# Row statistics moved from VectorE to additions and to ScalarE, and closer due times for the last graphs, in a planned four-layer graph network

## The chip, the core and the metric

The kernel runs on one core of a Trainium2 chip. The metric is the device time of one execution in microseconds (us). Before the change it is 2857.97 us, the median of three runs (2857.74 to 2859.51).

## The reference

There are 64 graphs. Each has 256 nodes with 512 features (`x`) and a 256 x 256 matrix of weights between nodes (`adj`), all float32. Every graph passes four layers, and each layer normalizes the rows of x, takes the positive part, and adds what the layer gives to x:

```
h = max(layernorm(x), 0);  x = x + L0(h, adj, W, a)      # attention, elu
h = max(layernorm(x), 0);  x = x + L1(h, adj, kernel, bias)
h = max(layernorm(x), 0);  x = x + L2(h, adj, kernel)
h = max(layernorm(x), 0);  x = x + L3(h, adj, W)
layernorm(x) = (x - mean) / sqrt(var + 1e-5)             # along a row
L0: e = leaky_relu(Wh1 + Wh2^T); att = softmax(where(adj > 0.5, e, -9e15), axis=1); elu(att @ Wh)
L1: An = dh * (adj + I) * dh, dh = 1/sqrt(rowsum(adj + I)); relu(An @ h @ kernel + bias)
L2: relu(adj @ h @ kernel) * mask, mask = 1 where a row of h has an entry that isn't 0
L3: agg = adj @ h / max(rowsum(adj), 1e-6); relu([h, agg] @ W^T)
```

## The kernel before, in words

A graph's 256 rows lie in two chunks of 128 partitions, so x is a tile `xs` of [128, 2, 512]. Its four quarters have keys of their own (`xs.00` to `xs.11`: chunk, then half of the columns).

Nothing in the source fixes the order of the work by loops alone. `graph(b)` (L341) only records operations: an engine, an estimated time, the keys it reads and writes, and a due time. A graph's last operations are due at `APART * b` (L343), and `Plan.place` (L69) walks back from there, so that each operation gets the due time that its heirs leave it. Then the planner places all operations one by one. Each engine takes the operation that can start first, then an urgent one, then the one that is due first. The estimates are multiplied by `STRETCH` (L25), a step from one engine to another is charged `HOP` = 0.25 us, and PE counts an operation as startable only `SPARE` (L26) after its operands are ready in the plan. Buffers are limited by the table at L782: seven tiles of x, three of h, eight banks of PSUM and so on. The operations are then emitted in the order of their planned starts, and on the chip every engine runs its own queue in that order. All transfers are issued from SP's queue.

Around that plan, the work of one graph is as follows.

- **Loads.** x and `a_nat`, the adjacency by rows (L367, L369), and the same adjacency in eight block transfers as `ab` (L567), from which VectorE (DVE) makes the transposed `aT` (L570).
- **Norm** (L372). For each chunk DVE takes `bn_stats` (L381) and `bn_aggr` (L383). GpSimd (POOL) adds the epsilon and takes the power -1/2 (L385, L387). DVE scales by the degree factor where asked (L390) and makes the bias `nb` (L392). ScalarE (ACT) writes `h` as a relu with scale and bias (L396).
- **Degrees** (L576 to L583). DVE sums `a_nat` by rows, POOL makes `dh`, DVE makes `rdeg`.
- **Attention.** DVE takes the logits as products with `wa` (L590), which is made once, at the start, from W and the two halves of `a` (L252 to L282). One half of the logits goes through DRAM and comes back spread along the rows as `pl` (L354 to L362). ACT adds the two (L596). DVE makes `off`, -9e15 where the adjacency is at most 0.5 (L601), the leaky relu (L603), the product with the comparison (L605), the sum with `off` (L607) and the negated row maximum (L610). ACT takes the exponential with its row sum (L614), DVE the reciprocal (L617) and the scaling of each chunk (L620).
- **Products.** `aggregate` (L424) multiplies h with the adjacency on TensorE (PE) into `pt`, the copies of which make seven left operands (L414 to L407). `project` (L485) takes seven products in three banks `pz`, `py`, `pv` (L503), with ACT copies (L542) and DVE additions (L544) out of PSUM between them. In the last layer there are two such projections, and h is transposed first: DVE turns blocks (L722), and 16 transfers put them in place as `hw` (L727).
- **Additions to x.** `elu0` (L626), `relu_add` (L669) and `masked` (L699) add a layer's result to x in three pieces: quarter 10, quarter 11 and the whole chunk 0.
- **Store** of x (L770).

At the start the weights come in as well. For the last layer PE transposes them (L325), and ACT copies them out of PSUM (L332); POOL makes sums of weights (L289).

Of the kernel before, what the change touches and what calls it, by code (L numbers as in the profile page):

```python
# [10 lines left out]
AF = mybir.ActivationFunctionType  # L11
ALU = mybir.AluOpType
AX = mybir.AxisListType

P = 128
Q = 32
BANK = 512
EPS_LN = 1e-5
EPS_DEG = 1e-6
ALPHA = 0.2  # L20
NEG_INF = -9000000000000000.0
HOP = 0.25
APART = 12.0

STRETCH = {"DVE": 1.06, "ACT": 1.1, "POOL": 1.1, "PE": 1.0, "DMA": 1.0}  # L25
SPARE = 0.8  # L26

# [121 lines left out]
def kernel(  # L149
# [21 lines left out]
    nc = tc.nc  # L171
    B, N, F = x.shape
    O = w0.shape[1]
    NC = N // P
# [14 lines left out]
    class Tiles:  # L189
# [5 lines left out]
        def declare(self, name, shape, pool=None, tag=None):  # L195
            tag = pool or tag or name
            self.tiles[name] = Buffered(shape, tag, f"{name}_{self.name}")
# [140 lines left out]
    def quarter(t, i, j):  # L338
        return t[:, i, j * OH : (j + 1) * OH]

    def graph(b):  # L341

        me = Tiles(str(b), APART * b)  # L343
        op, declare, together = me.op, me.declare, me.together

        def along(name, column, keys):
# [22 lines left out]
        op("DMA", 256, lambda g: nc.sync.dma_start(  # L369
            g["a_nat"], adj[b].rearrange("(c p) m -> p c m", p=P)), (), ["a_nat"])  # L370

        def norm(l, scale=None):  # L372

            st, mv, rs, nb, h = (f"{n}{l}" for n in ("stats", "mv", "rstd", "nb", "h"))
            declare(st, [P, NC, 6], tag="stats")
            declare(mv, [P, NC, 2], tag="mv")
            declare(rs, [P, NC], tag="rstd")
            declare(nb, [P, NC], tag="nb")
            declare(h, [P, NC, F], tag="h")
            for c in range(NC):  # L380
                op("DVE", 0.69, lambda g, c=c: nc.vector.bn_stats(g[st][:, c, :], g["xs"][:, c, :]),  # L381
                   XS[2 * c : 2 * c + 2], [f"{st}.{c}"])
                op("DVE", 0.18, lambda g, c=c: nc.vector.bn_aggr(g[mv][:, c, :], g[st][:, c, :]),  # L383
                   [f"{st}.{c}"], [f"{mv}.{c}"])
            op("POOL", 0.31, lambda g: nc.gpsimd.tensor_scalar_add(g[rs], g[mv][:, :, 1], EPS_LN),  # L385
               [f"{mv}.0", f"{mv}.1"], [rs])
            op("POOL", 0.72, lambda g: nc.gpsimd.tensor_tensor(g[rs], g[rs], minus_half, ALU.pow),  # L387
               [rs, "=half"], [rs])
            if scale is not None:
                op("DVE", 0.2, lambda g: nc.vector.tensor_tensor(g[rs], g[rs], g[scale], ALU.mult),  # L390
                   [rs, scale], [rs])
            op("DVE", 0.3, lambda g: nc.vector.scalar_tensor_tensor(  # L392
                g[nb], g[mv][:, :, 0], -1.0, g[rs], ALU.mult, ALU.mult),
               [f"{mv}.0", f"{mv}.1", rs], [nb])
            for c in range(NC):
                op("ACT", 0.81, lambda g, c=c: nc.scalar.activation(  # L396
                    g[h][:, c, :], g["xs"][:, c, :], AF.Relu, bias=g[nb][:, c : c + 1],
                    scale=g[rs][:, c : c + 1]), XS[2 * c : 2 * c + 2] + [nb, rs], [f"{h}.{c}"])
# [147 lines left out]
        def both(t):  # L546

            return t[:, 0:2].rearrange("p a o -> p (a o)")
# [3 lines left out]
        def pieces(l):  # L552
            kept = f"c{l}"
            return (
                (1, "xs.10", lambda g: g[f"pz{l}"], [f"pz{l}"], lambda g: quarter(g["xs"], 1, 0), ["xs.10"], 256),
                (1, "xs.11", lambda g: g[kept][:, 2], [f"{kept}.11"], lambda g: quarter(g["xs"], 1, 1), ["xs.11"], 256),
                (0, "xs.0", lambda g: both(g[kept]), [f"{kept}.00", f"{kept}.01"], lambda g: g["xs"][:, 0, :], ["xs.00", "xs.01"], 512),
            )


# [3 lines left out]
        for q in range(P // Q):  # L564
# [10 lines left out]
        norm(0)  # L575
        op("DVE", 0.67, lambda g: nc.vector.tensor_reduce(g["deg"], g["a_nat"], AX.X, ALU.add),  # L576
           ["a_nat"], ["deg"])
        op("POOL", 0.36, lambda g: nc.gpsimd.tensor_scalar_add(g["dh"], g["deg"], 1.0), ["deg"], ["dh"])
        op("POOL", 0.72, lambda g: nc.gpsimd.tensor_tensor(g["dh"], g["dh"], minus_half, ALU.pow),
           ["dh", "=half"], ["dh"])  # L580
        op("DVE", 0.18, lambda g: nc.vector.tensor_scalar_max(g["rdeg"], g["deg"], EPS_DEG),
           ["deg"], ["rdeg"])
        op("DVE", 0.18, lambda g: nc.vector.reciprocal(g["rdeg"], g["rdeg"]), ["rdeg"], ["rdeg"])  # L583
# [11 lines left out]
        for c in range(NC):  # L595
            op("ACT", 0.47, lambda g, c=c: nc.scalar.activation(  # L596
                g["e"][:, c, :], g["pl"], AF.Identity, bias=g["lg"][:, 1, c : c + 1]),
               ["pl", f"lg.1{c}"], [f"e.{c}"], urgent=True)
        E = ["e.0", "e.1"]
        declare("off", [P, NC, N])  # L600
        op("DVE", 0.48, lambda g: nc.vector.tensor_scalar(  # L601
            g["off"], g["aT"], 0.5, NEG_INF, ALU.is_le, ALU.mult), ["aT"], ["off"])
        op("DVE", 0.69, lambda g: nc.vector.scalar_tensor_tensor(  # L603
            g["e"], g["e"], ALPHA, g["e"], ALU.mult, ALU.max), E, E)
        op("DVE", 0.69, lambda g: nc.vector.scalar_tensor_tensor(  # L605
            g["e"], g["aT"], 0.5, g["e"], ALU.is_gt, ALU.mult), E + ["aT"], E)
        op("DVE", 0.69, lambda g: nc.vector.tensor_tensor(g["e"], g["e"], g["off"], ALU.add),  # L607
           E + ["off"], E)
        declare("top", [P, NC])
# [9 lines left out]
        for c in range(NC):  # L619
            op("DVE", 0.37, lambda g, c=c: nc.vector.tensor_scalar_mul(  # L620
                g["e"][:, c, :], g["e"][:, c, :], g["den"][:, c : c + 1]),
               [f"e.{c}", f"den.{c}"], [f"e.{c}", "e"])
        aggregate("h0", "e", 0)


        def elu0(i, key, y, y_keys, to, to_keys, n, tag):  # L626
            us = 0.42 if n == 256 else 0.61
            ex = f"ex{tag}"
            declare(ex, [P, n], tag=f"ex{n}")
            op("ACT", us, lambda g: nc.scalar.activation(g[ex], y(g), AF.Relu, scale=-1.0),  # L630
               y_keys, [ex], urgent="pz0" in y_keys)
            op("ACT", us, lambda g: nc.scalar.activation(g[ex], g[ex], AF.Exp, scale=-1.0), [ex], [ex])
            us = 0.43 if n == 256 else 0.69
            op("DVE", us, lambda g: nc.vector.scalar_tensor_tensor(
                to(g), y(g), 0.0, to(g), ALU.max, ALU.add), y_keys + to_keys, to_keys,
               urgent="pz0" in y_keys)
            op("DVE", us, lambda g: nc.vector.scalar_tensor_tensor(
                to(g), g[ex], -1.0, to(g), ALU.add, ALU.add), [ex] + to_keys, to_keys)

# [28 lines left out]

        def relu_add(i, key, y, y_keys, to, to_keys, n):  # L669
            op("DVE", 0.43 if n == 256 else 0.69, lambda g: nc.vector.scalar_tensor_tensor(  # L670
                to(g), y(g), 0.0, to(g), ALU.max, ALU.add), y_keys + to_keys, to_keys,
               urgent="pz3" in y_keys)

        first, second, third = pieces(1)

        def last1(pz):
            declare("v1", [P, OH], tag="ex256")
            op("DVE", 0.49, lambda g: scaled(g, 1, g["v1"], g[pz], 0), [pz, "dh", "=bias"], ["v1"], urgent=True)
            relu_add(1, "xs.10", lambda g: g["v1"], ["v1"], first[4], first[5], 256)

        project([Weighted("xw1", 1)], 1, scaled_keep, 0.49, scaled_total, last1, ["dh", "=bias"])
        relu_add(*second)
        relu_add(*third)
        norm(2)

# [12 lines left out]

        def masked(i, key, y, y_keys, to, to_keys, n, tag):  # L699
            v = f"v2{tag}"  # L700
            declare(v, [P, n], tag=f"ex{n}")
            op("ACT", 0.5 if n == 256 else 0.72, lambda g: nc.scalar.activation(
                g[v], y(g), AF.Relu, scale=g["mask"][:, i : i + 1]), y_keys + [f"mask.{i}"], [v],
               urgent="pz2" in y_keys)
            op("DVE", 0.43 if n == 256 else 0.69, lambda g: nc.vector.tensor_tensor(
                to(g), g[v], to(g), ALU.add), [v] + to_keys, to_keys)

# [53 lines left out]
        for at, to, i in ((2, S3, 1), (3, S4, 0)):  # L761
# [3 lines left out]
        project([Weighted("hw", 3), Gathered("aT", "aw", "y")], 3, plain_keep, 0.38, plain_total,  # L765
                lambda _: relu_add(*pieces(3)[0]))
        _, second, third = pieces(3)
        relu_add(*second)
        relu_add(*third)
        op("DMA", 512, lambda g: nc.sync.dma_start(  # L770
# [9 lines left out]
    for b in range(B):  # L780
        graph(b)
    buffers = dict(  # L782
        xs=7, a_nat=1, ab=1, aT=6, h=3, mva=6, xw=5, c=3, off=1, junk=1, ex256=2, ex512=2,
        wa_col=1, turned=1, row=4, pl=2, pr=1, hb=1, ps=8,
    )
    for tag in ("stats", "mv", "rstd", "nb", "deg", "dh", "rdeg", "lg", "top", "den", "mask"):
        buffers[tag] = 6
# [34 lines left out]
```

## Time and profile before

| | |
|---|---|
| median of three runs | 2857.97 us |
| the profiled execution | 2858.11 us |
| its span, first to last instruction | 2856.3 us |
| mean granted clock of PE | 0.998 |
| mean of one bn_stats / one bn_aggr on DVE | 0.681 / 0.163 us |
| mean of one relu of the norm on ACT | 0.811 us |
| stores of the last six graphs issued at | 2722.4, 2760.0, 2789.8, 2813.5, 2830.5, 2852.7 us |

The profile names an instruction by its line, its engine, its operation and "out<-in" with the program's tile names. Busy time is the time in which an engine executes. The chain that ended last follows the execution back from its last instruction to whatever released each step. A matmul of float32 leaves two records for each matmul in the source, so that the 101 matmuls of a graph are 202 records. A releaser in square brackets is what the profile infers to have ended the idle time before an instruction. The granted clock tells which part of full speed PE was given in a stretch.

### The profile page before, as it was taken

What the parts mean: (1) busy time and instruction counts of PE and PEld (TensorE: products, weight loads), DVE (VectorE), ACT (ScalarE), POOL (GpSimd) and SP (SyncE); (2) the same over time, 40 slices, a digit from 0 to 9 for tenths busy, and PEclk for the clock granted to TensorE, in tenths of its full rate; (3) what the DMA queues carried; (4) which work ended last, traced back from release to release, by engine and by line L of the source; (5) the groups of instructions that cost most, each with busy time, mean ns of one, the idle gap of its engine ahead of it and who ended that gap; (6) DMA issues with size and microseconds to landing.
All of it is one profiled execution on the core that took longest, in us unless ns stands there. A gap on an engine that the chain in (4) does not pass through costs nothing.

```text
span 2856.3 us, 41700 instructions
## 1 busy us (share of the span) xinstructions
PE 2807.5 (98%) x12968; PEld 2464.4 (86%) x12968; DVE 2317.2 (81%) x5904; ACT 1326.1 (46%) x2963; POOL 1098.4 (38%) x1691
## 2 busy tenths in 40 slices
PE   4999999999999999999999999999999999999998
PEld 3888888888888888888888888888888888888887
DVE  8888888888888888878888878888888888888764
ACT  4544444444454444444444444444444445444432
POOL 5443343343333433433433334434334344344331
PEclk9999999999999999999999999999999999999999
DMA  6122222222222222222222222222222222222111
GB/s 184 22 48 51 55 59 49 59 65 47 51 60 54 58 59 49 61 49 56 64 49 53 67 44 57 59 50 59 56 50 62 49 54 66 48 53 61 39 37 45
DMA packets 495052, 160.98 MB, mean 56 GB/s; under 512 B 424816, under 2 KB 460656, under 8 KB 494832
## 3 DMA queue, kind: packets, MB, share of 16 engines
q1 hardware_dynamic: 494832, 158.33, 23.5%
q8 instruction: 104, 1.70, 0.3%
q14 instruction: 116, 0.95, 0.1%
HBM read 90.96 MB, written 33.69 MB: 44 GB/s over the span
## 4 chain that ended last, share of the span: by engine, by line
PE 97%; DVE 1%; SPq 1%; DMA 1%; ACT 0%; issue 0%; POOL 0%; DVEq 0%; ACTq 0%; POOLq 0%
PE pz L503 42%; PE pt L434 23%; PE pv L503 21%; PE py L503 11%; SPq L727 0%; DMA xs<-in_x_dram 0%; DMA wb<-in_L_gnn_W_dram 0%; ACT h L396 0%; DVE e L605 0%; DVE e L607 0%; SPq L567 0%; ACT e L614 0%; DVE stats L381 0%; DVE xs L670 0%; DMA hw<-hb 0%
## 5 line engine op out<-in xcount | busy, mean ns | idle before, releaser
L503 PE MATMUL pz<-wb,xw 128*128 128x256 f32 x3072 | 752.5, 379 | 0.9 <-ACT c L542 0.9
L503 PEld LDWEIGHTS pz<-wb,xw 128*128 128x128 f32 x3072 | 583.4, 190 | 80.7 <-ACT c L542 1.3
L503 PE MATMUL pz<-wb,hw 128*128 128x256 f32 x2048 | 524.5, 379 | 5.8 <-DMA hw<-hb 3.5
L406 POOL TENSOR_TENSOR xw<-xw 128x256 f32<-128x256 f32 x384 | 300.7, 803 | 536.1 <-DVE xw L402 443.3
L542 ACT COPY c<-pz 128x256 f32<-128x256 f32 x576 | 212.8, 370 | 591.7 <-PE pz L503 575.0
L503 PEld LDWEIGHTS pz<-wb,hw 128*128 128x128 f32 x2048 | 388.6, 190 | 60.9 <-issue 3.9
L396 ACT ACTIVATE h<-xs,nb,rstd 128x512 f32<-128x512 f32 x512 | 401.3, 811 | 60.0 <-DVE nb L392 59.9
L503 PE MATMUL pv<-wb,xw 128*128 128x256 f32 x1536 | 394.0, 379 | 0.0
L385 POOL TENSOR_SCALAR rstd<-mv 128x2 f32<-128x2 f32 x256 | 98.3, 384 | 698.2 <-DVE mv L383 325.7
L381 DVE BATCH_NORM_STATS2 stats<-xs 128x6 f32<-128x512 f32 x512 | 340.9, 681 | 6.9 <-DMA xs<-in_x_dram 5.2
L503 PEld LDWEIGHTS pv<-wb,xw 128*128 128x128 f32 x1536 | 291.8, 190 | 39.7
L544 DVE TENSOR_TENSOR c<-pv,c 128x256 f32<-128x256 f32 x384 | 161.0, 420 | 151.5 <-PE pv L503 112.8
L503 PE MATMUL pv<-wb,hw 128*128 128x256 f32 x1024 | 263.7, 380 | 0.0
L434 PE MATMUL pt<-e,h 128*128 128x256 f32 x1024 | 243.0, 382 | 20.9 <-ACT e L596 20.9
L434 PE MATMUL pt<-ahT,h 128*128 128x256 f32 x1024 | 237.5, 382 | 2.9 <-ACT b_w L332 2.9
L434 PE MATMUL pt<-aT,h 128*128 128x256 f32 x1024 | 238.5, 379 | 0.0
L434 PEld LDWEIGHTS pt<-e,h 128*128 128x128 f32 x1024 | 195.6, 191 | 48.7 <-ACT e L596 21.1
L434 PEld LDWEIGHTS pt<-ahT,h 128*128 128x128 f32 x1024 | 196.4, 192 | 30.3 <-ACT b_w L332 3.1
L503 PEld LDWEIGHTS pv<-wb,hw 128*128 128x128 f32 x1024 | 195.1, 191 | 26.7
L542 ACT COPY y<-pz 128x256 f32<-128x256 f32 x192 | 71.2, 371 | 316.4 <-PE pz L503 311.5
L434 PEld LDWEIGHTS pt<-aT,h 128*128 128x128 f32 x1024 | 194.6, 190 | 26.4
L387 POOL TENSOR_TENSOR rstd<-rstd,minus_half 128x2 f32<-128x2 f32 x256 | 200.6, 784 | 21.3
(103 smaller groups left out, 4411.0 us busy)
## 6 DMA issues: line engine op xcount, KB each, us to landing
xs<-in_x_dram SPq DMA_DIRECT2D x64, 512.0 KB
hw<-hb SPq DMA_DIRECT2D x1024, 32.0 KB
out_dram<-xs SPq DMA_DIRECT2D x64, 512.0 KB
ab<-in_adj_dram SPq DMA_DIRECT2D x512, 32.0 KB
a_nat<-in_adj_dram SPq DMA_DIRECT2D x64, 256.0 KB
pl<-dpl SPq DMA_DIRECT2D x64, 128.0 KB
pr<-dpr SPq DMA_DIRECT2D x64, 128.0 KB
w3n_w<-in_L_gnn_W_dram SPq DMA_DIRECT2D x4, 512.0 KB
```

The costliest lines, as they stand in the source:

```text
L381: op("DVE", 0.69, lambda g, c=c: nc.vector.bn_stats(g[st][:, c, :], g["xs"][:, c, :]), XS[2 * c : 2 * c + 2], [f"{st}.{c}"])
L385: op("POOL", 0.31, lambda g: nc.gpsimd.tensor_scalar_add(g[rs], g[mv][:, :, 1], EPS_LN), [f"{mv}.0", f"{mv}.1"], [rs])
L387: op("POOL", 0.72, lambda g: nc.gpsimd.tensor_tensor(g[rs], g[rs], minus_half, ALU.pow), [rs, "=half"], [rs])
L396: op("ACT", 0.81, lambda g, c=c: nc.scalar.activation(g[h][:, c, :], g["xs"][:, c, :], AF.Relu, bias=g[nb][:, c : c + 1], scale=g[rs][:, c ...
L406: op("POOL", 0.85, lambda g, i=i, o=o: nc.gpsimd.tensor_tensor(g[xw][:, o], g[xw][:, i], g[xw][:, S2], ALU.subtract), put(i, S2), put(o), ...
L434: nc.tensor.matmul(g[pt][:, kk, :], lhsT=g[h][:, c, k * P : (k + 1) * P], rhs=g[moving][:, c, :], start=(c == 0), stop=(c == NC - 1),)
L503: nc.tensor.matmul(g[t], lhsT=o.left(g, left, k), rhs=o.right(g, right, k), start=start and n == 0, stop=n == len(parts) - 1, skip_group_c ...
L542: return "ACT", lambda g, to, block: nc.scalar.copy(to, block)
L544: plain_total = (0.43, lambda g, i, to, block: nc.vector.tensor_tensor(to, block, to, ALU.add))
```

## The change

The first norm of a graph stays with `bn_stats`. For the other three, each of the three additions to x also writes its row sum (`accum_out`) into a tile `total`. POOL makes the negated means from these. ACT squares the rows with the mean as bias and sums them on the way, POOL adds the epsilon, takes the power, scales by the degree factor and makes the bias. Chunk 1 now goes ahead of chunk 0.

The row sums of `a_nat` are taken by ACT, in copies in place. `off` becomes +0.5 or -0.5, and one minimum with `off` times 1.8e16 takes the place of the product and the sum. The scaling of the exponentials is done by ACT. The additions of `masked` become another kind of DVE instruction so that they can give sums.

In the planner, due times are 13 apart instead of 12, and 0.3 of that for the last three graphs. The factors of DVE and POOL and PE's reserve are changed, and so are a few buffer counts.

```diff
-APART = 12.0
-STRETCH = {"DVE": 1.06, "ACT": 1.1, "POOL": 1.1, "PE": 1.0, "DMA": 1.0}
-SPARE = 0.8
+APART = 13.0
+LAST, LATE = 3, 0.3
+STRETCH = {"DVE": 1.2, "ACT": 1.1, "POOL": 1.06, "PE": 1.0, "DMA": 1.0}
+SPARE = 0.15
...
-        me = Tiles(str(b), APART * b)
+        me = Tiles(str(b), APART * (b - (1.0 - LATE) * max(0, b - (B - 1 - LAST))))
...
+            else:
+                t = f"total{l}"
+                op("POOL", 0.3, lambda g: nc.gpsimd.tensor_scalar(
+                    g[mv][:, 0, 1:2], g[t][:, 1:2], g[t][:, 2:3], -1.0 / F, ALU.add, ALU.mult),
+                   [f"{t}.10", f"{t}.11"], [f"{mv}.m1"])
+                op("POOL", 0.3, lambda g: nc.gpsimd.tensor_scalar(
+                    g[mv][:, 0, 0:1], g[t][:, 0:1], -1.0 / F, None, ALU.mult), [f"{t}.0"], [f"{mv}.m0"])
+                for c in (1, 0):
+                    op("ACT", 1.0, lambda g, c=c: nc.scalar.activation(
+                        g[h][:, c, :], g["xs"][:, c, :], AF.Square, bias=g[mv][:, 0, c : c + 1],
+                        accum_out=g[mv][:, 1, c : c + 1]),
+                       XS[2 * c : 2 * c + 2] + [f"{mv}.m{c}"], [f"{h}.{c}", f"{mv}.v{c}"])
+                op("POOL", 0.31, lambda g: nc.gpsimd.tensor_scalar(
+                    g[rs], g[mv][:, 1], 1.0 / F, EPS_LN, ALU.mult, ALU.add),
+                   [f"{mv}.v0", f"{mv}.v1"], [rs])
...
+                op("POOL", 0.3, lambda g: nc.gpsimd.tensor_tensor(g[rs], g[rs], g[scale], ALU.mult),
...
+                op("POOL", 0.3, lambda g: nc.gpsimd.tensor_tensor(
+                    g[nb], g[mv][:, 0], g[rs], ALU.mult), [f"{mv}.m0", f"{mv}.m1", rs], [nb])
...
+        def into_x(l, key, at, us, fn, reads, to_keys, urgent=False):
+
+            t = f"total{l + 1}"
+            sums = l < 3
+            op("DVE", us + (0.1 if sums else 0.0), lambda g: fn(
+                g, dict(accum_out=g[t][:, at : at + 1]) if sums else {}),
+               reads + to_keys, to_keys + ([f"{t}.{key}"] if sums else []), urgent=urgent)
...
-        op("DVE", 0.67, lambda g: nc.vector.tensor_reduce(g["deg"], g["a_nat"], AX.X, ALU.add),
-           ["a_nat"], ["deg"])
+        for c in range(NC):
+            op("ACT", 0.66, lambda g, c=c: nc.scalar.activation(
+                g["a_nat"][:, c, :], g["a_nat"][:, c, :], AF.Copy, accum_out=g["deg"][:, c : c + 1]),
+               [f"a_nat.{c}"], [f"a_nat.{c}", f"deg.{c}"])
...
-            g["off"], g["aT"], 0.5, NEG_INF, ALU.is_le, ALU.mult), ["aT"], ["off"])
+            g["off"], g["aT"], 0.5, 0.5, ALU.is_gt, ALU.subtract), ["aT"], ["off"])
...
-            g["e"], g["aT"], 0.5, g["e"], ALU.is_gt, ALU.mult), E + ["aT"], E)
-        op("DVE", 0.69, lambda g: nc.vector.tensor_tensor(g["e"], g["e"], g["off"], ALU.add),
-           E + ["off"], E)
+            g["e"], g["off"], -2.0 * NEG_INF, g["e"], ALU.mult, ALU.min), E + ["off"], E)
...
-            op("DVE", 0.37, lambda g, c=c: nc.vector.tensor_scalar_mul(
-                g["e"][:, c, :], g["e"][:, c, :], g["den"][:, c : c + 1]),
+            op("ACT", 0.5, lambda g, c=c: nc.scalar.activation(
+                g["e"][:, c, :], g["e"][:, c, :], AF.Copy, scale=g["den"][:, c : c + 1]),
...
-        xs=7, a_nat=1, ab=1, aT=6, h=3, mva=6, xw=5, c=3, off=1, junk=1, ex256=2, ex512=2,
-        wa_col=1, turned=1, row=4, pl=2, pr=1, hb=1, ps=8,
+        xs=7, a_nat=1, ab=1, aT=6, h=3, mva=6, xw=5, c=3, off=2, junk=1, ex256=3, ex512=1,
+        wa_col=1, turned=1, row=4, pl=1, pr=1, hb=1, ps=8,
```

More of the change, by code (lines that the diff above doesn't have):

```diff
@@ L369, in graph @@
         op("DMA", 256, lambda g: nc.sync.dma_start(
-            g["a_nat"], adj[b].rearrange("(c p) m -> p c m", p=P)), (), ["a_nat"])
+            g["a_nat"], adj[b].rearrange("(c p) m -> p c m", p=P)), (), ["a_nat.0", "a_nat.1"])
         def norm(l, scale=None):
-            st, mv, rs, nb, h = (f"{n}{l}" for n in ("stats", "mv", "rstd", "nb", "h"))
-            declare(st, [P, NC, 6], tag="stats")
-            declare(mv, [P, NC, 2], tag="mv")
+            mv, rs, nb, h = (f"{n}{l}" for n in ("mv", "rstd", "nb", "h"))
+            declare(mv, [P, 2, NC], tag="mv")
             declare(rs, [P, NC], tag="rstd")
@@ L379, in norm @@
             declare(h, [P, NC, F], tag="h")
[L380 to L386, printed above, removed]
+            if l == 0:
+                declare("stats", [P, NC, 6])
+                for c in range(NC):
+                    op("DVE", 0.69, lambda g, c=c: nc.vector.bn_stats(
+                        g["stats"][:, c, :], g["xs"][:, c, :]), XS[2 * c : 2 * c + 2], [f"stats.{c}"])
+                    op("DVE", 0.18, lambda g, c=c: nc.vector.bn_aggr(
+                        g[mv].rearrange("p a c -> p c a")[:, c, :], g["stats"][:, c, :]),
+                       [f"stats.{c}"], [f"{mv}.m{c}", f"{mv}.v{c}"])
+                op("POOL", 0.31, lambda g: nc.gpsimd.tensor_scalar(
+                    g[rs], g[mv][:, 1], EPS_LN, None, ALU.add), [f"{mv}.v0", f"{mv}.v1"], [rs])
+                sign = -1.0
+            else:
[10 more added lines that the diff above has]
+                       XS[2 * c : 2 * c + 2] + [f"{mv}.m{c}"], [f"{h}.{c}", f"{mv}.v{c}"])
+                op("POOL", 0.31, lambda g: nc.gpsimd.tensor_scalar(
+                    g[rs], g[mv][:, 1], 1.0 / F, EPS_LN, ALU.mult, ALU.add),
+                   [f"{mv}.v0", f"{mv}.v1"], [rs])
+                sign = 1.0
             op("POOL", 0.72, lambda g: nc.gpsimd.tensor_tensor(g[rs], g[rs], minus_half, ALU.pow),
@@ L389, in norm @@
             if scale is not None:
-                op("DVE", 0.2, lambda g: nc.vector.tensor_tensor(g[rs], g[rs], g[scale], ALU.mult),
+                op("POOL", 0.3, lambda g: nc.gpsimd.tensor_tensor(g[rs], g[rs], g[scale], ALU.mult),
                    [rs, scale], [rs])
[L392 to L395, printed above, removed]
+            if l == 0:
+                op("DVE", 0.22, lambda g: nc.vector.scalar_tensor_tensor(
+                    g[nb], g[mv][:, 0], sign, g[rs], ALU.mult, ALU.mult),
+                   [f"{mv}.m0", f"{mv}.m1", rs], [nb])
+            else:
+                op("POOL", 0.3, lambda g: nc.gpsimd.tensor_tensor(
+                    g[nb], g[mv][:, 0], g[rs], ALU.mult), [f"{mv}.m0", f"{mv}.m1", rs], [nb])
+            for c in (0, 1) if l == 0 else (1, 0):
                 op("ACT", 0.81, lambda g, c=c: nc.scalar.activation(
@@ L553, in pieces @@
             kept = f"c{l}"
+            if l < 3:
+                declare(f"total{l + 1}", [P, 3], tag="total")
             return (
-                (1, "xs.10", lambda g: g[f"pz{l}"], [f"pz{l}"], lambda g: quarter(g["xs"], 1, 0), ["xs.10"], 256),
-                (1, "xs.11", lambda g: g[kept][:, 2], [f"{kept}.11"], lambda g: quarter(g["xs"], 1, 1), ["xs.11"], 256),
-                (0, "xs.0", lambda g: both(g[kept]), [f"{kept}.00", f"{kept}.01"], lambda g: g["xs"][:, 0, :], ["xs.00", "xs.01"], 512),
-            )
+                (1, "10", lambda g: g[f"pz{l}"], [f"pz{l}"], lambda g: quarter(g["xs"], 1, 0), ["xs.10"], 256, 1),
+                (1, "11", lambda g: g[kept][:, 2], [f"{kept}.11"], lambda g: quarter(g["xs"], 1, 1), ["xs.11"], 256, 2),
+                (0, "0", lambda g: both(g[kept]), [f"{kept}.00", f"{kept}.01"], lambda g: g["xs"][:, 0, :], ["xs.00", "xs.01"], 512, 0),
+            )
+        def into_x(l, key, at, us, fn, reads, to_keys, urgent=False):
[4 more added lines that the diff above has]
+               reads + to_keys, to_keys + ([f"{t}.{key}"] if sums else []), urgent=urgent)
         declare("ab", [P, NC, N], tag="ab")
@@ L575, in graph @@
         norm(0)
-        op("DVE", 0.67, lambda g: nc.vector.tensor_reduce(g["deg"], g["a_nat"], AX.X, ALU.add),
-           ["a_nat"], ["deg"])
-        op("POOL", 0.36, lambda g: nc.gpsimd.tensor_scalar_add(g["dh"], g["deg"], 1.0), ["deg"], ["dh"])
+        for c in range(NC):
+            op("ACT", 0.66, lambda g, c=c: nc.scalar.activation(
+                g["a_nat"][:, c, :], g["a_nat"][:, c, :], AF.Copy, accum_out=g["deg"][:, c : c + 1]),
+               [f"a_nat.{c}"], [f"a_nat.{c}", f"deg.{c}"])
+        op("POOL", 0.36, lambda g: nc.gpsimd.tensor_scalar_add(g["dh"], g["deg"], 1.0), ["deg.0", "deg.1"], ["dh"])
         op("POOL", 0.72, lambda g: nc.gpsimd.tensor_tensor(g["dh"], g["dh"], minus_half, ALU.pow),
@@ L581, in graph @@
         op("DVE", 0.18, lambda g: nc.vector.tensor_scalar_max(g["rdeg"], g["deg"], EPS_DEG),
-           ["deg"], ["rdeg"])
+           ["deg.0", "deg.1"], ["rdeg"])
         op("DVE", 0.18, lambda g: nc.vector.reciprocal(g["rdeg"], g["rdeg"]), ["rdeg"], ["rdeg"])
@@ L619, in graph, with elu0 @@
         for c in range(NC):
-            op("DVE", 0.37, lambda g, c=c: nc.vector.tensor_scalar_mul(
-                g["e"][:, c, :], g["e"][:, c, :], g["den"][:, c : c + 1]),
+            op("ACT", 0.5, lambda g, c=c: nc.scalar.activation(
+                g["e"][:, c, :], g["e"][:, c, :], AF.Copy, scale=g["den"][:, c : c + 1]),
                [f"e.{c}", f"den.{c}"], [f"e.{c}", "e"])
         aggregate("h0", "e", 0)
-        def elu0(i, key, y, y_keys, to, to_keys, n, tag):
+        def elu0(i, key, y, y_keys, to, to_keys, n, at, tag):
             us = 0.42 if n == 256 else 0.61
@@ L636, in elu0 @@
                urgent="pz0" in y_keys)
-            op("DVE", us, lambda g: nc.vector.scalar_tensor_tensor(
-                to(g), g[ex], -1.0, to(g), ALU.add, ALU.add), [ex] + to_keys, to_keys)
+            into_x(0, key, at, us, lambda g, kw: nc.vector.scalar_tensor_tensor(
+                to(g), g[ex], -1.0, to(g), ALU.add, ALU.add, **kw), [ex], to_keys)
         first, second, third = pieces(0)
@@ L667, in graph, with relu_add @@
             to, block, g["dh"][:, i : i + 1], to, ALU.mult, ALU.add))
[L669 to L672, printed above, removed]
+        def relu_add(l, i, key, y, y_keys, to, to_keys, n, at):
+            into_x(l, key, at, 0.43 if n == 256 else 0.69,
+                   lambda g, kw: nc.vector.scalar_tensor_tensor(
+                       to(g), y(g), 0.0, to(g), ALU.max, ALU.add, **kw), y_keys, to_keys,
+                   urgent="pz3" in y_keys)
         first, second, third = pieces(1)
@@ L678, in last1 @@
             op("DVE", 0.49, lambda g: scaled(g, 1, g["v1"], g[pz], 0), [pz, "dh", "=bias"], ["v1"], urgent=True)
-            relu_add(1, "xs.10", lambda g: g["v1"], ["v1"], first[4], first[5], 256)
+            relu_add(1, 1, "10", lambda g: g["v1"], ["v1"], first[4], first[5], 256, 1)
         project([Weighted("xw1", 1)], 1, scaled_keep, 0.49, scaled_total, last1, ["dh", "=bias"])
-        relu_add(*second)
-        relu_add(*third)
+        relu_add(1, *second)
+        relu_add(1, *third)
         norm(2)
@@ L697, in graph, with masked @@
         aggregate("h2", "aT", 2)
-        def masked(i, key, y, y_keys, to, to_keys, n, tag):
+        def masked(i, key, y, y_keys, to, to_keys, n, at, tag):
             v = f"v2{tag}"
@@ L704, in masked @@
                urgent="pz2" in y_keys)
-            op("DVE", 0.43 if n == 256 else 0.69, lambda g: nc.vector.tensor_tensor(
-                to(g), g[v], to(g), ALU.add), [v] + to_keys, to_keys)
+            into_x(2, key, at, 0.43 if n == 256 else 0.69,
+                   lambda g, kw: nc.vector.scalar_tensor_tensor(
+                       to(g), g[v], 0.0, to(g), ALU.add, ALU.add, **kw), [v], to_keys)
         first, second, third = pieces(2)
@@ L765, in graph @@
         project([Weighted("hw", 3), Gathered("aT", "aw", "y")], 3, plain_keep, 0.38, plain_total,
-                lambda _: relu_add(*pieces(3)[0]))
+                lambda _: relu_add(3, *pieces(3)[0]))
         _, second, third = pieces(3)
-        relu_add(*second)
-        relu_add(*third)
+        relu_add(3, *second)
+        relu_add(3, *third)
         op("DMA", 512, lambda g: nc.sync.dma_start(
@@ L782 @@
     buffers = dict(
-        xs=7, a_nat=1, ab=1, aT=6, h=3, mva=6, xw=5, c=3, off=1, junk=1, ex256=2, ex512=2,
-        wa_col=1, turned=1, row=4, pl=2, pr=1, hb=1, ps=8,
+        xs=7, a_nat=1, ab=1, aT=6, h=3, mva=6, xw=5, c=3, off=2, junk=1, ex256=3, ex512=1,
+        wa_col=1, turned=1, row=4, pl=1, pr=1, hb=1, ps=8,
     )
-    for tag in ("stats", "mv", "rstd", "nb", "deg", "dh", "rdeg", "lg", "top", "den", "mask"):
+    for tag in ("stats", "total", "mv", "rstd", "nb", "deg", "dh", "rdeg", "lg", "top", "den", "mask"):
         buffers[tag] = 6
```

## Prediction

> **What bounds the kernel now.** I read the engines' busy time first, then the chain that ended last, then tables by stretch, then the timeline where PE is idle. The page's busy time and chain by engine:
>
> ```profile
> span 2856.3 us, 41700 instructions
> ...
> PE 2807.5 (98%) x12968; PEld 2464.4 (86%) x12968; DVE 2317.2 (81%) x5904; ACT 1326.1 (46%) x2963; POOL 1098.4 (38%) x1691
> ...
> PE 97%; DVE 1%; SPq 1%; DMA 1%; ACT 0%; issue 0%; POOL 0%; DVEq 0%; ACTq 0%; POOLq 0%
> ```
>
> PE is the bound, and the change touches no matmul. The table by stretch (start:end, length, then busy time and count of PE, PEld, DVE, ACT and POOL, the granted clock, DMA share, GB/s) shows where PE loses anything:
>
> ```profile
> 0.00:36.40 36.40, 3.77 (x9) 1.48 (x9) 26.38 (x63) 9.70 (x17) 19.18 (x28) 1.00 0.74 216
> ...
> 60.62:66.04 5.42, 2.13 (x17) 1.69 (x17) 5.28 (x12) 5.39 (x13) 0.00 (x0) 0.88 0.08 29
> 66.04:72.31 6.27, 6.27 (x17) 5.09 (x18) 5.35 (x14) 1.88 (x6) 5.69 (x5) 0.56 0.08 22
> ...
> 200.00:2816.50 2616.50, 2616.50 (x12124) 2303.29 (x12123) 2132.90 (x5470) 1223.03 (x2732) 994.35 (x1550) 1.00 0.23 54
> 2816.50:2851.43 34.93, 29.14 (x120) 23.11 (x119) 12.08 (x25) 5.77 (x14) 3.33 (x4) 0.95 0.14 31
> 2851.43:2856.30 4.87, 0.01 (x1) 0.00 (x0) 1.12 (x2) 0.00 (x0) 0.00 (x0) 1.00 0.29 108
> ```
>
> From 200 to 2816.5 PE is never idle: 2616.5/12124 = 0.2158 us a record, 202 records or 43.6 us a graph. Nothing that eases DVE there can show. What can be won lies at the ends. **Start:** no real matmul before 36.40. **Stall:** from 60.62 PE is idle 5.42 - 2.13 = 3.3 us, and the 17 records after it take 6.27 instead of 3.67 us at clock 0.56, 2.6 more; with idle times of 0.56 near 91 and 0.86 at 167, 7.3 us. **Tail:** 120 records need 25.9 of 34.93 us, so 9.0 is lost. The 4.9 us after the last matmul (an addition, the store) stay. The first two, in the timeline:
>
> ```profile
> 35.04 2.48 DVE L620 TENSOR_SCALAR e<-e,den 128x256 f32<-128x256 f32 x2
> ...
> 36.06 1.31 POOL L289 TENSOR_TENSOR wb<-wb 128x512 f32<-128x512 f32 x1
> ...
> 36.40 6.10 PE L434 MATMUL pt<-e,h 128*128 128x256 f32 x16 [20.85 <-ACT e L596]
> ...
> 65.63 0.35 ACT L332 COPY b_w<-pw_w 128x256 f32<-128x256 f32 x1
> ...
> 66.04 6.43 PE L434 MATMUL pt<-ahT,h 128*128 128x256 f32 x16 [2.90 <-ACT b_w L332]
> ```
>
> PE starts when the first L620 is done, on DVE. The stall ends with an ACT copy queued behind relus and exponentials. The tail:
>
> ```profile
> 2819.20 11.15 SPq L727 DMA_DIRECT2D hw<-hb  x16
> ...
> 2832.22 1.34 PE L503 MATMUL pz<-wb,hw 128*128 128x256 f32 x4 [3.48 <-DMA hw<-hb]
> ...
> 2848.58 1.13 PE L503 MATMUL pz<-wb,hw 128*128 128x256 f32 x4 [0.46 <-ACT c L542]
> ```
>
> The last graph's 16 transposing transfers take SP 11.15 us, and the next-to-last graph's work is too short to cover them; then it runs alone, with five idle times of 0.46 from here back to 2823.85.
>
> **Steady engines, per graph (counts by mean rows).** DVE loses 6 bn_stats x 0.681 + 6 bn_aggr x 0.163 + 3 nb x 0.175 + scale 0.14 + degree 0.67 + one of L605/L607 0.81 + 2 L620 x 0.483 = 8.2 us. It gains nine accumulator reads, bounded below by none and above by 0.11; L590's read row gives 0.081, taken: 0.7. So 36.2 - 7.5 = 28.7. ACT gains 6 Squares: L396's 0.811 plus L689's read 0.192 = 1.0, from below L689's 0.722 + 0.192; degrees 2 x (0.505 + 0.19) and scaling 2 x 0.505 by L614's row: 8.4, so 20.7 + 8.4 = 29.1. POOL gains ten tiny operations between 0.317 (L578) and 0.78 (L387, a power); a plain product is nearer L385's 0.386, so 3.9: 17.2 + 3.9 = 21.1. All stay under PE's 43.6, which hides them: zero. Were the cover gone, an engine's excess over 43.6 would count 64 times. The mask's other form, one or two more buffers of off and ex256, and the new additions in place of L705 (0.713 against 0.682) are zero for the same reason.
>
> **The lengthened wait.** A later norm was bn_stats, bn_aggr, two POOL steps, nb, relu: 0.68 + 0.16 + 0.39 + 0.78 + 0.17 + 0.81 = 3.0 us. It becomes POOL mean, Square, add, power, nb, relu: 0.39 + 1.0 + 0.39 + 0.78 + 0.39 + 0.81 = 3.8, plus 0.39 where the degree scales. Behind a Square that waits stand ACT's PSUM copies, for which PE waits; behind the POOL means stand the operand sums L406. ACT's relus already waited 59.9 us for nb, and POOL 326 us for bn_aggr, with no idle PE in the middle, since a graph takes long (the first from its load at 1.2 to its store at 203.1) and so some 4 to 5 are under way. At the ends it is some 1 us a layer.
>
> **Start, -2.3.** The first graph's chain loses L607 (0.82), the degree ahead of it (0.68), and its first scaling goes from 1.24 on DVE (half of 2.48) to 0.505 on ACT. Here a rule speaks against the change: the Trainium skill, ScalarE: Activation LUTs, Rules for kernel authors, keeps plain multiplications on VectorE. By L620's median, 0.354, moving costs 0.15 and the start gains 1.35; by the row of this place, with POOL's weight sums beside it, it gains 0.73 and the start 2.2 to 2.3. The row decides. Ends: 0.8, if the scaling queues behind the two relus that stood on ACT there (1.5), and 4.6, if the chain follows the landing of pl at 26.26 at once (0.91 + 0.69 + 0.78 + 0.69 + 1.2 + 0.14 + 0.5, some 0.6 of gaps). One moved cost is covered: with one buffer of ex512 the second half of a is loaded after four L269 products, near 12 instead of 4 us, and SP holds what is queued behind it. Landing 5 to 7 us later, as the first did (2.22 to 9.1), its products, turns and logits (2.8 + 1.1 + 1.6) end near 24, still under pl's 26.26; otherwise it costs some 3. pl's single buffer is free: its read ended at 27.2, the next issue was at 30.13.
>
> **Stall, -2.** From 10 to 100 us DVE is busy 83.8 of 90; the rows of that window take out 8 L620 (6.5), 4 L607 (3.8), 3 degrees (2.0), 6 later bn_stats with their rest (6), so 17 net of 1. That could remove all 7.3. But ACT, 14.2 of 16 us busy from 50 to 66 and the one that ends the stall, gets four Squares, and the norm is longer: from below, 4 us worse. The Trainium skill, SBUF — State Buffer, Who interferes with whom, adds that a DVE operation with two SBUF inputs waits for a POOL operation reading SBUF. L605 shows it: 0.977 in this window, 0.769 later. By the rule ten new POOL operations could hold DVE 3.9 us a graph; by the row, which grew under 1.3 us sums, less. I take 2, near the middle.
>
> **Tail, -5.5.** Due times 3.9 apart instead of 12 keep four graphs level. SP needs 11.2 us a graph, PE 70 records x 0.2158 = 15.1 in the last layer, so SP is not late next. The 3.48 wait with its cold clock (13 records in 4.5 us, 1.7 more) goes, and some of the 0.46 waits: 5.5. Ends: 0, if the last graph still ends alone or loses in the longer norm; 8, if only its own last waits remain.
>
> **Sum.** 2858.1 (the profiled execution: span 2856.3 and 1.8 around it, 0.1 above the median) - 2.3 - 2 - 5.5 = 2848.3, against the median 2848.2.
>
> **Rivals.** *Both ends close* (0.14): 4.6 + 7.3 + 8 = 19.9, so 2838; DVE's 17 us speak for it, ACT at the stall against. *The gain is hidden* (0.12): the relieved engine isn't the late one, or the due times do nothing, as stores already came 23.7 and 16.9 apart. Start -0.8, stall +4, tail -3: 2858. *Waits in the middle, slower* (0.08): PE's reserve in the plan falls from 0.8 to 0.15, PE runs in order, and POOL's means are planned at 0.32 where rows say 0.39. One 0.46 wait a graph over 60 graphs is 28 us: 2876; it decides from 0.16 us a graph. Against it: the plan gives a PSUM copy 0.25 + 0.42 + 0.25 = 0.92, the trace 0.46 idle. A Square outside the loaded table, of which the trace shows one load of 1.283, would be a like cost; no run here shows one.
>
> **Numbers.** The likeliest case has 0.66, with 2842 to 2852. About 0.2%, 5.7 us, is what can be told from no change: faster (below 2852.3) 0.80, same 0.12, slower 0.08. The range, 2836 to 2859, leaves out the slower rival and the edges.
>
> **Signs.** The start: first pt matmul near 34. The stall: an idle time and a clock dip before 75. The tail: hw transfers of several graphs closer together, no wait of 3 us near the end. The middle: idle near zero, DVE near 66% busy, ACT 67%. PE idle between 200 and 2800 above 10 us, or ACT table loads, would make it wrong.

## The result and the profile after

The changed kernel takes 2846.58 us (median of five runs, 2845.21 to 2847.17), the kernel before beside it 2857.74. The ratio is 0.9962, with a 95% interval of 0.9948 to 0.9975: 11.2 us less. The forecast was 2848.2, 9.8 less than before. The profiled execution has a span of 2845.3 us, 11.0 shorter.

The page after, by the same parts as before:

```profile
span 2845.3 us, 42816 instructions
...
PE 2803.4 (99%) x12968; PEld 2462.3 (87%) x12968; DVE 1968.7 (69%) x5200; ACT 1700.9 (60%) x4115; POOL 1256.9 (44%) x2331
...
PE 98%; DMA 1%; DVE 0%; SPq 0%; ACT 0%; issue 0%; DVEq 0%
```

The work moved as the diff says: DVE lost 348 us, ACT gained 375, POOL 158. PE stays the bound. The table by stretch shows where the 11 us came from:

```profile
0.00:35.72 35.72, 3.76 (x8) 1.45 (x8) 24.55 (x58) 9.54 (x23) 15.85 (x24) 1.00 0.77 224
35.72:200.00 164.28, 158.45 (x724) 136.26 (x725) 121.79 (x324) 117.45 (x299) 98.77 (x167) 0.99 0.27 66
200.00:2816.50 2616.50, 2616.50 (x12125) 2303.33 (x12124) 1811.41 (x4796) 1570.19 (x3785) 1139.87 (x2138) 1.00 0.23 54
...
2816.50:2840.50 24.00, 24.00 (x113) 21.06 (x112) 9.90 (x23) 3.72 (x10) 2.37 (x3) 1.00 0.17 65
2840.50:2845.30 4.80, 0.67 (x4) 0.24 (x2) 0.99 (x2) 0.00 (x0) 0.00 (x0) 0.96 0.29 109
```

Counted in one stretch from 0 (a record on a boundary of the table stands in both rows), PE has 12855 records up to 2816.5, and before it had 12849. So at that point the changed kernel is only 6 records, 1.3 us, ahead. The other 9.7 us are won after it: 24 us without a gap, where there had been 34.93 with 5.8 idle. The list of all that PE waited for has nothing from the tail:

```profile
PE pw_l L244 <- DVE junk_l L270: 17.9, 6, 9.5
PE pt L460 <- ACT e L657: 13.8, 1, 13.8
PE pw_w L326 <- DMA w3n_w<-in_L_gnn_W_dram: 2.1, 1, 2.1
PE pz L529 <- ACT c L568: 2.0, 2, 1.4
PE pz L529 <- DVE c L696: 1.5, 1, 1.5
```

The first row belongs to the preparation of the logit weights. The second is the start, the others lie between 46 and 87 us. At the start ACT's timeline shows what ended the wait:

```profile
32.22 0.19 ACT L651 ACTIVATION_READ_ACCUMULATOR e<-e,top 128x1 f32 x1
34.37 0.42 ACT L613 ACTIVATE a_nat<-a_nat 128x256 f32<-128x256 f32 x1 [1.96 <-DMA a_nat<-in_adj_dram]
...
35.18 0.89 ACT L657 ACTIVATE e<-e,den 128x256 f32<-128x256 f32 x2
```

The first graph's exponentials are done at 32.4, and its reciprocal stands on DVE at 33.27. Then ACT waits for the transfer of the next graph's `a_nat`, because that graph's degree copies (L613) are ahead of the first graph's scaling (L657) in its queue. There is one buffer for `a_nat`, so that transfer is issued only when the first graph's own copies are done. The chain shows both steps:

```profile
27.67 0.58 ACT a_nat L613 x3
28.26 0.03 ACT e L634
28.28 6.06 DMA a_nat<-in_adj_dram
...
34.69 0.58 ACT a_nat L613 x3
35.27 0.41 ACT e L657
```

### The profile page after: what moved, and what is told of

The parts are those of the page before. It is cut to its first block, busy times and chain, and to the rows that moved or that the text cites. A ratio compares the mean times of both kernels' runs of the same rounds, so it can differ in the third digit from the quotient of the medians.

```text
span 2845.3 us, 42816 instructions
## 1 busy us (share of the span) xinstructions
PE 2803.4 (99%) x12968; PEld 2462.3 (87%) x12968; DVE 1968.7 (69%) x5200; ACT 1700.9 (60%) x4115; POOL 1256.9 (44%) x2331
## 4 chain that ended last, share of the span: by engine, by line
PE 98%; DMA 1%; DVE 0%; SPq 0%; ACT 0%; issue 0%; DVEq 0%
PE pz L529 43%; PE pt L460 23%; PE pv L529 21%; PE py L529 11%; DMA a_nat<-in_adj_dram 0%; DMA xs<-in_x_dram 0%; DMA w3n_w<-in_L_gnn_W_dram 0%; DMA dpl<-tpl 0%; PE pw_w L326 0%; SPq L259 0%; SPq L603 0%; DMA ab<-in_adj_dram 0%; DVE e L644 0%; ACT h L422 0%; ACT a_nat L613 0%
## 5 line engine op out<-in xcount | busy, mean ns | idle before, releaser
L432 POOL TENSOR_TENSOR xw<-xw 128x256 f32<-128x256 f32 x384 | 320.1, 851 | 264.8 <-DVE xw L428 186.3
L401 ACT ACTIVATE h<-xs,mv 128x512 f32<-128x512 f32 x384 | 277.0, 722 | 66.0 <-POOL mv L398 35.7
L460 PE MATMUL pt<-e,h 128*128 128x256 f32 x1024 | 233.5, 381 | 13.8 <-ACT e L657 13.8
L460 PEld LDWEIGHTS pt<-ahT,h 128*128 128x128 f32 x1024 | 194.5, 190 | 26.6 <-ACT xw L440 0.2
L628 DVE SCALAR_TENSOR_TENSOR e<-h,wa 128x512 f32<-128x512 f32 x256 | 188.0, 735 | 34.4 <-PE pt L460 21.3
L409 POOL TENSOR_TENSOR rstd<-rstd,minus_half 128x2 f32<-128x2 f32 x256 | 195.8, 765 | 21.1
L529 PE MATMUL py<-wb,xw 128*128 128x256 f32 x768 | 197.2, 379 | 0.0
```

Of the source, the lines that this page charges most:

```text
L401: op("ACT", 1.0, lambda g, c=c: nc.scalar.activation(g[h][:, c, :], g["xs"][:, c, :], AF.Square, bias=g[mv][:, 0, c : c + 1], accum_out=g[ ...
L432: op("POOL", 0.85, lambda g, i=i, o=o: nc.gpsimd.tensor_tensor(g[xw][:, o], g[xw][:, i], g[xw][:, S2], ALU.subtract), put(i, S2), put(o), ...
L460: nc.tensor.matmul(g[pt][:, kk, :], lhsT=g[h][:, c, k * P : (k + 1) * P], rhs=g[moving][:, c, :], start=(c == 0), stop=(c == NC - 1),)
L529: nc.tensor.matmul(g[t], lhsT=o.left(g, left, k), rhs=o.right(g, right, k), start=start and n == 0, stop=n == len(parts) - 1, skip_group_c ...
L628: op("DVE", 0.77, lambda g, j=j, c=c: nc.vector.scalar_tensor_tensor(g["e"].rearrange("p c n -> p (c n)"), g["h0"][:, c, :], 1.0, wa[:, j, ...
```

## The experiments

At first I held that the closer due times made the gain, at the tail. The rival was that the lighter engines made it. All ratios are to the kernel before on the same chip, with 95% intervals.

**Due times alone** in the kernel before:

```diff
-        me = Tiles(str(b), APART * b)
+        me = Tiles(str(b), APART * (b - (1.0 - LATE) * max(0, b - (B - 1 - LAST))))   # APART 12, LAST 3, LATE 0.3
```

> The kernel before with nothing but the closer due times (12 apart, the last three graphs 0.3 of that). Theory, the due times make the gain at the end: the 9.0 us that PE loses after 2816 go for the greater part, so 2848 to 2850, with no idle time over 1 us in the last 40 us, and a start and a stall at the head as before. Rival, the lighter engines make the gain: the tail keeps most of its waits, since each graph still has the same work on DVE, and the time is 2855 to 2858.

Measured: 2853.97, ratio 0.9989 (0.9983 to 0.9996). That is 3 us, between the two. The last wait for transfers is gone, but PE's timeline has new waits where the level graphs come together, the longest on DVE's scaling L621. From 2660 to 2700 PE is busy for 37.3 us, where it was for all 40.0 before:

```profile
2682.01 1.13 PE L504 MATMUL pz<-wb,xw 128*128 128x256 f32 x4 [0.46 <-ACT c L543]
2683.60 1.13 PE L504 MATMUL pz<-wb,xw 128*128 128x256 f32 x4 [0.46 <-ACT c L543]
2687.37 3.72 PE L435 MATMUL pt<-e,h 128*128 128x256 f32 x16 [1.77 <-DVE e L621]
```

**The changed kernel without closer due times** (LATE 1.0):

> The changed kernel with all due times 13 apart, the last ones too. Theory, the due times make the gain: the waits at the end come back, so 2855 to 2857, 9 to 10 us above the changed kernel; the head is as in the changed kernel, a first pt matmul near 35.7. Rival, the lighter engines make the gain: 2847 to 2849.

Measured: 2854.80, 0.9993 (0.9985 to 1.0001). The wait for hw is back in PE's timeline, with the same five idle times of 0.46:

```profile
2829.10 1.78 PE L529 MATMUL pz<-wb,hw 128*128 128x256 f32 x4 [3.22 <-DMA hw<-hb]
```

So in the changed kernel the due times are worth 0.9993 - 0.9962 = 0.31%, 9 us. The order of PE's instructions in these two kernels is the same for the first nine tenths. Yet up to 200 us this execution did 740 records and the changed kernel's 732, so 1.7 us at the head vary between executions. One difference is PE's granted clock: in the changed kernel's execution it is 0.53 from 49.2 to 52.7, in this one 1.00 throughout the head.

**The plan without the moved work** and **the moved work without the plan**. The first has before's operations under all new constants and buffer counts:

> The operations of before under the changed kernel's plan: its due times, factors, reserve of PE and buffer counts. Theory, the due times make the gain and PE's small reserve costs nothing: 2847 to 2851, idle PE between 200 and 2800 below 2 us. Rival, the heavier DVE of before needs the larger reserve: waits of 0.4 to 1 us at PE in the middle, 2860 or more.

Measured: 3101.72, 1.0861 (1.0846 to 1.0876). Both expectations are missed by far. PE waits about once a graph at the same place, as its timeline shows:

```profile
1043.24 1.84 PE L504 MATMUL pz<-wb,xw 128*128 128x256 f32 x4 [2.31 <-ACT c L543]
1091.10 1.91 PE L504 MATMUL pz<-wb,xw 128*128 128x256 f32 x4 [2.31 <-ACT c L543]
```

A graph takes 47.86 us here instead of 43.6. Before's DVE work, 36.2 us by the trace, is 43.4 with the new factor of 1.2, as much as PE's. I take the plan to be limited by DVE, but that is not shown: reserve and due times alone do no such harm (below), and no run here separates the factors from the distance of 13 and the buffer counts. The second has the moved work and new buffers under before's factors, reserve and due times:

> The operations and buffer counts of the changed kernel, but before's due times (12 apart throughout), factors and reserve of PE. Theory, moving work off DVE is worth about 1 us at the head and nothing behind 200: 2855 to 2858, with waits at the end as before. Rival, the moved work is what counts: 2846 to 2850.

Measured: 2873.94, 1.0061 (1.0046 to 1.0077), slower than before and outside both expectations. PE starts at 32.85, earlier than in either kernel, but then has stalls of 5.3, 5.7 and 4.7 us:

```profile
65.31 5.50 PE L460 MATMUL pt<-ahT,h 128*128 128x256 f32 x16 [5.34 <-ACT h L422]
...
105.42 5.92 PE L460 MATMUL pt<-ahT,h 128*128 128x256 f32 x16 [5.70 <-ACT b_w L333]
...
153.98 5.41 PE L460 MATMUL pt<-ahT,h 128*128 128x256 f32 x16 [4.72 <-ACT h L422]
```

It did 641 records up to 200 us, 86 fewer than before. My theory, that the moved work matters little, fell with this pair: it needs constants of the new plan, and the new plan as a whole needs it.

**The plan's constants one at a time**, in the changed kernel. First PE's reserve, SPARE back at 0.8:

> The changed kernel with PE's reserve back at 0.8. Theory, the factors and not the reserve repaired the head: within 2 us of the changed kernel, 2845 to 2849. Rival, the reserve is what does it: stalls of 5 us at PE before 160 us, as with all old plan constants, 2855 to 2865.

Measured: 2855.20, 0.9994 (0.9986 to 1.0002), 9 us slower than the changed kernel, as the rival had it. The two profiled executions differ by 7.0 us. Of these 4.7 are lost at the head (710 records up to 200 us, 22 fewer), where a stall like that of before is back. The rest is lost at the tail, where two idle times of 0.46 remain:

```profile
68.71 5.89 PE L460 MATMUL pt<-ahT,h 128*128 128x256 f32 x16 [4.51 <-ACT wb L333]
...
2842.48 1.13 PE L529 MATMUL pz<-wb,hw 128*128 128x256 f32 x4 [0.46 <-ACT c L568]
...
2844.50 1.13 PE L529 MATMUL pz<-wb,hw 128*128 128x256 f32 x4 [0.46 <-ACT c L568]
```

Then the factors, STRETCH back at DVE 1.06 and POOL 1.1:

> The changed kernel with the old factors (DVE 1.06, POOL 1.1). Theory, at the factor 1.06 the plan puts DVE's operations earlier than they run, ACT's relus and exponentials queue behind what is late, and PE stalls at the head: 2855 to 2868, with waits for h before 160 us. Rival, the factors are indifferent where DVE has a third of its time free: 2845 to 2849.

Measured: 2972.73, 1.0404 (1.0390 to 1.0418), far worse than the theory had it, and for another place: PE's waits are in the middle, for the scaled exponentials, once in about two graphs. This is the row of its list of PE's waits (total, times, longest):

```profile
PE pt L460 <- ACT e L657: 86.9, 29, 11.3
```

**The degrees, where the start was lost.** Back on DVE:

```diff
-        for c in range(NC): op("ACT", 0.66, ... AF.Copy, accum_out=g["deg"][:, c : c + 1]) ...
+        op("DVE", 0.67, lambda g: nc.vector.tensor_reduce(g["deg"], g["a_nat"], AX.X, ALU.add), ...
```

> The changed kernel with the degrees summed by DVE again (one reduction a graph). Theory, the start gained only 0.7 instead of 2.3 us because ACT's queue holds the next graph's degree copies, which wait for a_nat until 34.34, in front of the first scaling: with them gone PE starts 1 to 2 us earlier, near 34, and if nothing else is late the time is 2844 to 2846. Rival, the first softmax is late for another reason (DVE's own queue), so that the start stays near 35.5 and the time at 2846 to 2848.

Still on ACT, but recorded behind the graph's own scaling (and reading its key `e` in the plan):

> The changed kernel with the degrees still on ACT, but recorded behind the graph's own scaling, so that the plan puts them later in ACT's queue. Theory as for the degrees on DVE: start near 34, 2844 to 2846. Rival, the same as there, or the later dh delays the second layer's products: start near 35.5, or a new wait before 100 us, 2847 to 2850.

Measured: 2906.54, 1.0172 (1.0159 to 1.0186), and 2854.13, 0.9992 (0.9984 to 1.0). The start did come earlier, at 33.14 and 34.28 instead of 35.72, but neither kernel is faster for it, against both theories. With the degrees behind the scaling a stall of 5.68 us came back at 71. With the degrees on DVE another order of the same work arose, in which PE waits in the middle, around 1000 us about every 89 us. Its timeline, of POOL, ACT and PE:

```profile
1047.84 0.26 POOL L395 TENSOR_SCALAR mv<-total 128x1 f32<-128x1 f32 x1
...
1048.13 0.72 ACT L401 ACTIVATE h<-xs,mv 128x512 f32<-128x512 f32 x1 [1.38 <-POOL mv L395]
...
1048.86 0.89 ACT L655 ACTIVATE e<-e,den 128x256 f32<-128x256 f32 x2
...
1049.40 3.72 PE L460 MATMUL pt<-e,h 128*128 128x256 f32 x16 [1.67 <-ACT e L655]
```

A Square waits for POOL's mean, itself behind two sums of adjacency blocks on POOL, and behind the Square stands the scaling that PE needs. This is the added wait of the prediction, and here it costs.

**Reserve alone, then reserve and due times, in the kernel before**, with no operation moved:

> The kernel before with nothing changed but PE's reserve, 0.15 instead of 0.8. Theory, the smaller reserve shortens the stall at the head (it was worth some 6 us there in the changed kernel) and the tail is as before: 2850 to 2854, if the heavier DVE doesn't bring waits into the middle. Rival, with DVE at 81% the smaller reserve puts PE in front of operands that come late, each graph or every other graph: 2870 or more, with waits for the scaled exponentials between 200 and 2700.

> The kernel before with the reserve of 0.15 and the closer due times, no operation moved. Theory, the moved work is needed at the tail, where four level graphs put four softmaxes on DVE at once: 2 to 4 us below the kernel with the reserve alone, and 4 or more above the changed kernel's 2846.6. Rival, reserve and due times are the whole gain: 2845 to 2848.

Measured: 2858.96, 1.0007 (0.9999 to 1.0015), and 2849.50, 0.9973 (0.9963 to 0.9984). Neither the theory nor the rival of the first holds: the small reserve is worth nothing alone, and it brings no waits into the middle. With the due times it gives 7.7 us, more than the 3 of the due times alone, mainly since the wait at 2687 is gone (PE is busy for all 40.0 us from 2660 to 2700). That is 1.5 us short of the rival, reserve and due times as the whole gain. All waits of PE over 1 us in this kernel are at or before 104:

```profile
PE pt L435 <- DVE e L621: 21.3, 2, 20.8
PE pw_l L244 <- DVE junk_l L270: 10.5, 5, 8.9
PE pt L435 <- ACT h L397: 2.1, 1, 2.1
PE pz L504 <- DVE xw L403: 1.9, 1, 1.9
```

One idle time of 0.46 is left at the tail. So the moved work isn't needed to close it nearly: the smaller reserve with the due times does it too.

**Due times 14 apart** in the changed kernel:

> The changed kernel with due times 14 apart instead of 13. Theory, the plan is rugged: the sum of all work is the same, but another order of the same work gives 2 to 60 us more through waits at PE in the middle or at the head; 2848 or more. Rival, the distance is indifferent, 2845 to 2848.

Measured: 3125.09, 1.0936 (1.0921 to 1.0951). It is the theory's direction, but more than four times the size that it allowed. The wait every 95 us in the middle is a circle through the queues of PE and ACT, as the chain shows:

```profile
1093.11 2.17 PE pz L529 x10
1095.31 0.47 ACT v2a L740
1095.78 0.61 ACT v2c L740
1096.39 0.81 ACT e L634 x2
1097.22 0.73 DVE e L642
...
1100.80 0.52 ACT e L657
...
1101.36 5.73 PE pt L460 x16
```

An ACT operation waits for PE's latest product; a whole softmax stands behind it on ACT, and PE's next instruction needs that softmax.

## Why the prediction was right

**Bound and place: right.** PE is the bound in both kernels, is never idle from 200 to 2816.5 in either, and all of the gain lies at the ends.

**Start, forecast -2.3, measured -0.7.** The step that failed is the degree in the first graph's chain (0.68), and with it the claim that the loading of `a` is covered. The degree, which I counted only as taken off DVE, went into ACT's queue and waits there for its transfer.

From the first addition of pl to the last exponential it did get shorter, 28.16 to 32.4 instead of 26.26 to 34.2. Of these 3.7 us the two terms that I counted, L607 and the degree, are 1.5. Most of the rest is order: DVE starts the leaky relu as soon as the addition is done (29.05 and 29.09), where before other work stood between (27.17 and 29.96).

But the addition comes 1.9 us later. The second half of `a`, issued at 13.53, was done with its products at 21.4. Its copy `wa` ended only at 25.2, since ACT had a relu of the next graph ahead of it, which waited until 23.96. So the first graph's last logit ended at 27.06, not near 24, and later than pl's 26.26 of before. In the two runs with the degrees elsewhere the addition waits for this logit, as here with the degrees on DVE:

```profile
27.64 0.91 ACT L632 ACTIVATE e<-pl,lg 128x256 f32<-128x256 f32 x2 [1.14 <-DVE e L626]
```

The other 1.1 us, to 28.16, are the first graph's degree copies. Those of the next graph then hold the scaling to 35.18, 1.8 us after its reciprocal. I had asked what queues behind a Square, and for the start only for two relus ahead of the scaling. With the degrees elsewhere the start was 33.14 and 34.28, on both sides of the 34.1 forecast. In the kernel with the moved work and the old plan the copies stay on ACT, but behind the addition (26.39), and PE starts at 32.85. So it is their place in the queue that costs, not the move itself. That the start still fell near my lower end of 0.8 is luck: that end was worked out from the relus.

**Stall, forecast -2: too large.** The wait for `b_w` is gone, but waits of 1.4, 2.1, 0.6 and 1.5 us at 46, 49, 71 and 86 came in its place, with the clock at 0.53 after the second. Start and stall together won 1.1 to 1.3 us in the profiled execution, against 4.3 forecast. Executions with the same order of work differ as much: up to 200 us the kernel before did 727 records, and with closer due times, which change its order only behind 2570 us, 732. By the medians it is some 2 us (the kernel without closer due times, 0.9993, with no difference inside its interval). That DVE's relief ends the stall is not what the runs show: with the larger reserve the moved work has one of 4.51 us. The smaller reserve with before's operations also ends the wait for `b_w`, and gains nothing at the head (721 records up to 200 us).

**Tail, forecast -5.5, measured -9.7.** Right in mechanism, too small: I left some of the last graph's own 0.46 waits standing, and none remained, so that the gain lies beyond my far end of 8. The last four stores are issued at 2815.3, 2819.2, 2834.3 and 2841.7, so that the last two are 7.3 us apart instead of 22.2, and the last graph is alone only at the very end. What I did not see is that the due times need a partner, the small reserve or the new plan with the moved work; in the kernel before they gave 3 us alone.

**Steady engines.** Zero was right for all moved work in the middle of this kernel. DVE fell to 30.8 us a graph, not 28.7, ACT rose to 26.6 instead of 29.1, POOL to 19.6 instead of 21.1. ACT's Squares took 0.722 and their read 0.191, the lower end, and the degree copies 0.414. Two DVE operations with two SBUF inputs got longer, L603's from 0.718 to 0.820 and L750's from 0.448 to 0.622, and a third, L402's, shorter, from 0.457 to 0.433. The moved work under the old plan has the same POOL operations, and there the three took 0.678, 0.626 and 0.455. So more POOL work as such doesn't decide it, and these rows neither confirm nor refute the rule on the shared port that the prediction used.

**The slower rival** did not come in this kernel. Its mechanism, waits of PE in the middle, did in four neighbours. All four have the reserve of 0.15, which I named, but with before's operations and the rest of before's plan that reserve is harmless. It took another change of order, by the factors, a moved degree, one more microsecond of distance, or before's operations under the whole plan, and then they are 60 to 280 us slower than the changed kernel. None of the four was run with 0.8, so the reserve's part in it is not shown. My price, one wait of 0.46 a graph, was too low: the waits in the middle are 1.7 to 6.1 us in the timelines around 1000 us.

The bound and the place of the gain were right by reasoning. That the sum came within 1.6 us is luck: the tail's surplus of 4.2 us covers the 3.0 that start and stall lack. Of the 11.2 us, 7.7 come with reserve and due times alone, without any moved work (0.9973). The remaining 3 (0.9962) belong to the moved work, the factors, the distance and the buffers together. The two intervals overlap, and the head varies by 1.7 us, so how these 3 divide, and whether the moved work gains anything by itself, stays open. No run here beats the changed kernel.

## What to carry to other kernels

When one engine is busy 98% of the span, list its idle stretches first; moving work off another engine can at most earn those. When an operation moves to another engine, ask what it will wait for there, and what stands behind it: here copies that wait for a transfer cost the start 1.4 to 2.6 us (35.72 against 34.28 and 33.14). In a planned order the operations, their assumed costs and the reserve are one thing: change one of them at a time, and measure the whole. The two halves of this change, operations and plan, cost 16 and 244 us by themselves, while two of its constants alone, reserve and due times, gave most of the gain.

## What was not expected of the hardware

A short wait of PE can cost nearly twice its length. With before's operations under the new plan, PE is idle once a graph for 2.31 us, and the chain there shows the matmuls after it running slower:

```profile
1091.10 1.91 PE pz L504 x4
1093.01 4.36 PE pt L435 x16
```

The granted clock is 0.55 in the first of these two stretches and 0.80 in the second. In the middle of the changed kernel 16 such records take 3.45 us. A graph is 4.3 us longer for a wait of 2.31. Not every such wait costs this: in the changed kernel with the old factors PE waits 2.78 us at 1037 and at 1129, and the 16 records after it take 5.41 us the first time and 3.72 the second.

Tiny DVE operations can double without any change of their own: the [128, 2] comparison of the mask took 0.148 us in the middle of the kernel before and 0.309 in that of the changed kernel. More POOL work is not the reason by itself, since with the same POOL operations under the old plan it took 0.169. What each of them met is not shown.
